# Cross-attention block with MLP: VectorE's transposes in a row, and the plan of the fills dealt anew

## The chip, the cores and the metric

One core of a Trainium2 chip runs the whole kernel in one launch. The metric is the device time of the launch in microseconds. Everything is float32.

## The reference

Four batches of 512 query rows and 512 context rows, width 512, 16 heads of 32, an MLP of 2048:

```python
x = layer_norm(hidden, ln1_w, ln1_b)
q = (x @ q_w + q_b)          # 16 heads of 32
k = (ctx @ k_w + k_b)
v = (ctx @ v_w + v_b)
scores = einsum('bhqd,bhkd->bhqk', q, k) * scale   # masked keys get the lowest float
out = einsum('bhqk,bhkd->bhqd', softmax(scores), v)
hidden = out @ cproj_w + cproj_b + hidden
y = layer_norm(hidden, ln2_w, ln2_b)
y = gelu_tanh(y @ fc_w + fc_b)
return hidden + (y @ proj_w + proj_b)
```

## The kernel before

**Units, halves, blocks.** A unit `w` is one batch and one group of four heads, so there are 16 units, four to a batch. A block `p` is half a unit: 256 of its 512 query rows. The 32 blocks p0 to p31 run one after the other. In a block (`block`, L279) TensorE makes eight score tiles (`scores`, L254; two tiles of 128 query rows by four heads, each 128x512 in a PSUM bank of its own). VectorE adds the mask and takes the row minimum of the negated scores (`soften`, L265), ScalarE takes the exponential with its row sums (L269), and VectorE transposes the result in 32x32 squares, two heads at a time (`turn`, L277: four such instructions of 128x1024 to a block), and last the reciprocals of the sums (L300).

**Exchange.** The squares are then moved between partitions: GpSimd copies the four quarters that stay where they are (L329), and twelve DMAs carry the other twelve (L335). They are all issued on SyncE's queue; only for the last block every second row of them is issued on ScalarE's. `attend` (L338) multiplies the exchanged probabilities by V two or three blocks later, and VectorE scales the result into `oT` (L357).

**Fills.** What else the kernel has to do is dealt out by hand to the blocks: `put(p, ...)` lists the pieces of block p, and `block` calls `fill(0)`, `fill(1)` and `fill(2)` at three places. A piece has a cost: 3.4 (`CHAIN`) for a chain of matmuls (K, Q or V of a unit, one row tile of the output projection `cproj`, or of the MLP's second product `proj`), 5.95 for a pair of columns of the MLP's first product (`fc_by_pair`, seven products in place of eight), 0.5 for a transpose by TensorE and 0 for loads, statistics and normalizations. `fill(0)` and `fill(1)` take pieces up to a budget of 3.4, where a piece still fits when half its cost does; `fill(2)` takes the rest. So each engine has one fixed order of instructions: the order in which the program names them. Every piece of a fill stands in it between the block's own instructions, on VectorE, ScalarE, GpSimd and SyncE too.

**First layer norm.** For the batches 1 to 3 its three parts (`x2`: two of statistics, one of normalization; `ln1`, L178) and its four transposes (`x3`, `ln1_turn`) are pieces as well. For the batches 1 and 2 ScalarE does the normalization (L145) and copies the transposes out of PSUM (L163).

**MLP weights.** Eight slots of 256 KB form a ring. `load_mlp` (L449) loads the next weight on SyncE's queue as soon as the weight that is in its slot has been used for the last time; the list `weights` gives the order and the last use. `fc_sums` (L532) then lets GpSimd add up the blocks of a pair's weights. The gelus of a pair (L525) follow its last sum directly, on ScalarE.

**Beginning and end.** Ahead of p0 the kernel loads, normalizes batch 0 and makes K, V and Q of unit 0 (L876 to L908). Behind p31 come the rest of the MLP pieces, the last two `attend`s, `cproj` of batch 3 and the remaining MLPs (`last_mlps`), which the change leaves as they are.

Of the kernel before, what the change touches and what calls it, by code (L numbers as in the profile page):

```python
# [12 lines left out]
F32 = mybir.dt.float32  # L13
# [7 lines left out]
P = 128  # L21
# [29 lines left out]
def xattn_block(ctx: ExitStack, tc: tile.TileContext, x, encT, mask, q_w, k_w, v_w, c_w, fc_w, p_w, vecs, rows, out):  # L51
# [60 lines left out]

    S = {}
# [108 lines left out]
    def prep_q(w):  # L222
        b, g = divmod(w, NG)
        qT = k_q(w, 1)
        acc = acc_tile(f"accq_{w}")
        for d in range(ND):
            nc.tensor.matmul(acc, S["wq", w][:, d, :], xT[:, d, :], start=(d == 0), stop=(d == ND - 1))  # L227
        load_w(w + 2, names=("wq",))

        nc.scalar.activation(qT, acc, AF.Identity, bias=qb[:, g : g + 1], scale=-scale)  # L230
        S["qT", w] = qT
# [47 lines left out]
    def block(w, half, fill):  # L279

        q0, q1 = 2 * half, 2 * half + 1
        if half == 0:
            S["sums", w] = small.tile([P, NT, HG], F32, tag="sums", name=f"sums_{w}")
        tb = S["tb", w, half] = two.tile([P, NI, PW + 2 * HD], F32, tag="tb", name=f"tb_{w}_{half}")
        scores(w, q0)
        scores(w, q1)
        soften(w, q0, 0, 1, 2, 3)
        soften(w, q1, 0, 1)
        turn(w, q0, 0)
        soften(w, q1, 2, 3)  # L290
# [9 lines left out]
        nc.vector.transpose(  # L300
            tb[:, :, PW:].rearrange("p j (a q) -> p a j q", a=2), rr.rearrange("p a h d -> p (a h d)")
        )
# [18 lines left out]
    def copies(w, half):  # L321
# [8 lines left out]
        for d in range(1, NI):  # L330
            for i in (0, 2, 1, 3):
                j = (i + d) % NI

                q = nc.scalar if w == NW - 1 and half and i % 2 else nc.sync
                q.dma_start(out=pT[ts(j, HD), i], in_=tb[ts(i, HD), j])  # L335
        S["pT", w, half] = pT
# [89 lines left out]
    def ln2_turn(b, d):  # L426
# [4 lines left out]

    weights, products = [], []
    all_k = range(FQ)
    steps = [(n, 0, q, all_k) for n, q in (
        ("fc", 0), ("fc", 1), ("p", 0), ("fc", 2), ("p", 1), ("fc", 3), ("p", 2)
    )]
    steps += [
        ("fc", SPLIT, 0, (0, 1)), ("p", 0, 3, all_k), ("fc", SPLIT, 0, (2, 3)), ("fc", SPLIT, 1, all_k),
        ("p", SPLIT, 0, all_k), ("p", SPLIT, 1, all_k),
    ]  # L440
    for name, b, q, ks in steps:
        for n, k in enumerate(ks):
            last = len(products) + (n if name == "fc" else NT - 1)
            weights.append((name, b, q * FQ + k, last))
        products += [(name, b, q, k) for k in ks]

# [47 lines left out]

    def fc_seven(b, c, g, a, s, half):

# [12 lines left out]
        product(q1[:, 0], a[0][:, 0:2], y11)  # L509
        nc.scalar.copy(p1, q1[:, 0])  # L510
        product(q26[:, 0], a[0][:, 2:4], y21)
        product(q26[:, 1], s2, t2)
# [8 lines left out]
        add(nc.vector, g[:, 1:3], q34, g[:, 1:3])  # L521
        for i in range(2):
            f = 2 * c + i
            h = g[:, 2 * i : 2 * i + 2]
            nc.scalar.activation(h, h, AF.Gelu_apprx_tanh, bias=vec[:, FCB + f : FCB + f + 1], scale=1.0)  # L525

# [17 lines left out]
    def fc_by_pair(b, c):  # L544
        q, k = divmod(2 * c, FQ)
        fc_seven(b, c, gT[q % 2][:, k : k + 2, :], raw_pair(b, c), S["ws", b, c], acc_half)
        count[1] += 2
        count[4] += 1
        load_mlp()
        fc_sums()  # L550

    def proj(b, q, t):
        acc = acc_tile(f"accp_{b}_{q}_{t}")
        for k in range(FQ):
# [300 lines left out]

    def FC(b, q):
        return [(2 * CHAIN * 7 / 8, lambda c=c: fc_by_pair(b, c)) for c in range(q * FQ // 2, (q + 1) * FQ // 2)]

    def PJ(b, q):
        return [(CHAIN, lambda t=t: proj(b, q, t)) for t in range(NT)]  # L860

    def inputs(b):
# [28 lines left out]
    load_w(1, nc.sync, ("wv", "wq"))  # L891

    load_mlp()

# [5 lines left out]
    run(turns1(0))  # L900
    x1, x2, x3, x4 = inputs(1)
    run(x1)
# [8 lines left out]
    mlp = []  # L911
    mlp += FC(0, 0) + FC(0, 1) + PJ(0, 0) + FC(0, 2) + PJ(0, 1) + FC(0, 3) + PJ(0, 2)
    mlp += FC(SPLIT, 0)[:1] + PJ(0, 3) + FC(SPLIT, 0)[1:] + FC(SPLIT, 1) + PJ(SPLIT, 0) + PJ(SPLIT, 1)

# [31 lines left out]
    def put(p, *work, before=()):  # L946
# [33 lines left out]
    put(14, [q], some(2))  # L980
    put(15, some(2), x2[1:2], some(2))

    k, q, v = A(11)
    put(16, h_(1, 0, 1), x2[2:], [k, q], x3[:2], some(2), x3[2:3])
    put(17, [v], x3[3:], h_(1, 2, 3), x4, cb(1), C(1))
# [35 lines left out]
    exchange()  # L1021

# [61 lines left out]
```

## Time and profile before

| what | value |
|---|---|
| time, median of 3 runs | 776.24 us (775.86 to 776.32) |
| the profiled execution | 776.39 us |
| its span from the first to the last instruction | 774.6 us |
| granted TensorE clock, mean | 0.999 |
| VectorE busy | 622.6 us, 80% of the span |
| ScalarE busy | 338.4 us, 44% |
| GpSimd busy | 298.7 us, 39% |

All times below are microseconds from the first instruction of the profiled execution. A row of the chain of waits has start, duration and what ran; a row of the timeline has start, duration, engine, line, instruction, output and inputs, and in brackets the idle time of the engine before it with what ended it. SPq and ACTq are the queues on which SyncE and ScalarE issue DMAs; the duration is then that of issuing. One matmul of float32 counts as two instructions.

### The profile page before, as it was taken

To read this page: it belongs to the slowest core of one execution; us is meant where nothing else is said; L and a number is where in the kernel's file an instruction comes from. 1 tells how busy PE (TensorE), PEld (TensorE's weight loads), DVE (VectorE), ACT (ScalarE), POOL (GpSimd) and SP (SyncE) were. 2 spreads that over 40 slices of the span, in tenths; PEclk is the share of its full clock that TensorE was granted. 3 is DMA by queue.
4 is the path that set the end of the run, shared out by engine and by line. 5 is a ranking of instruction groups with operands and counts; after the bars stand their busy time and mean duration, and the time that the engine had idled before them with its cause. 6 is when DMAs were issued, how large, how long until landed. Compare 5 with 4: busy or idle time off the path is not lost.

```text
span 774.6 us, 12975 instructions
## 1 busy us (share of the span) xinstructions
PE 767.5 (99%) x4442; PEld 519.3 (67%) x4442; DVE 622.6 (80%) x1262; ACT 338.4 (44%) x760; POOL 298.7 (39%) x311
## 2 busy tenths in 40 slices
PE   9999999999999999999999999999999999999998
PEld 6655555467754745565554556446888889988897
DVE  3798999787988857877887889877878999679863
ACT  2577767477774626547663567401201221012200
POOL 1435446377355364224573553350060024300052
PEclk9999999999999999999999999999999999999999
DMA  8978778457766766664656586783523330023001
GB/s 329 309 223 216 183 200 229 125 151 177 224 167 162 183 181 169 156 173 121 162 136 189 144 240 167 207 254 122 199 84 98 90 115 14 28 83 95 1 16 41
DMA packets 54818, 119.37 MB, mean 154 GB/s; under 512 B 10417, under 2 KB 13617, under 8 KB 54625
## 3 DMA queue, kind: packets, MB, share of 16 engines
q1 hardware_dynamic: 53424, 114.88, 53.3%
q0 software_dynamic: 896, 2.82, 1.2%
q10 hardware_dynamic: 432, 0.86, 0.5%
q8 instruction: 35, 0.57, 0.3%
q14 instruction: 31, 0.25, 0.1%
HBM read 58.22 MB, written 6.82 MB: 84 GB/s over the span
## 4 chain that ended last, share of the span: by engine, by line
PE 96%; DVE 2%; DMA 1%; SPq 0%; issue 0%; ACT 0%; ACTq 0%; POOL 0%; DVEq 0%; POOLq 0%
PE q L507 25%; PE accp L555 9%; PE sc L259 8%; PE accv L239 8%; PE acck L217 7%; PE r L645 7%; PE accq L227 7%; PE av L352 7%; PE accc L392 7%; PE q4p L682 2%; PE q1p L700 2%; PE tp L158 2%; PE q2p L682 1%; DMA xe<-tb 1%; DVE tb L277 1%; PE warm L888 1%
## 5 line engine op out<-in xcount | busy, mean ns | idle before, releaser
L269 ACT ACTIVATE ptt<-ptt,mn 128x512 f32<-128x512 f32 x256 | 181.6, 710 | 125.8 <-DVE mn L265 125.8
L265 DVE CUSTOM_DVE_ANT_0 ptt<-sc,mb 128x512 f32<-128x512 f32 x256 | 161.5, 687 | 21.5 <-PE sc L259 16.9
L277 DVE STREAM_TRANSPOSE tb<-ptt 128x1024 f32<-128x1024 f32 x128 | 155.1, 1221 | 0.0
L329 POOL COPY pT<-tb 32x1088 f32<-32x1088 f32 x96 | 104.3, 1087 | 52.8 <-DVE oT L357 32.8
L555 PE MATMUL accp<-pbt,gt 128*128 128x512 f32 x192 | 85.1, 597 | 0.0
L507 PE MATMUL q<-yT,gt 128*128 128x256 f32 x320 | 78.9, 379 | 0.0
L259 PE MATMUL sc<-pbt 32*128 32x512 f32 x512 | 70.7, 616 | 1.5 <-ACT pbt L230 0.8
L555 PEld LDWEIGHTS accp<-pbt,gt 128*128 128x128 f32 x192 | 35.7, 190 | 47.6 <-issue 39.7
L507 PEld LDWEIGHTS q<-yT,gt 128*128 128x128 f32 x320 | 60.8, 190 | 8.7 <-issue 0.5
L525 ACT ACTIVATE ga<-ga,vec 128x512 f32<-128x512 f32 x40 | 26.7, 714 | 87.9 <-DVE ga L467 87.9
L239 PEld LDWEIGHTS accv<-ptt,xe 128*128 128x128 f32 x512 | 59.0, 192 | 8.4 <-DVE mn L265 5.3
L507 PE MATMUL q<-ys,gt 128*128 128x256 f32 x240 | 61.7, 379 | 0.0
L239 PE MATMUL accv<-ptt,xe 128*128 128x128 f32 x512 | 60.2, 276 | 0.0
L217 PE MATMUL acck<-xe,ptt 128*128 128x512 f32 x128 | 58.7, 601 | 0.0
L227 PE MATMUL accq<-xe,ptt 128*128 128x512 f32 x128 | 58.2, 597 | 0.0
L392 PE MATMUL accc<-wc,oT 128*128 128x512 f32 x128 | 56.1, 595 | 0.0
L507 PEld LDWEIGHTS q<-ys,gt 128*128 128x128 f32 x240 | 45.5, 190 | 6.6 <-DVE gt L464 0.4
L259 PEld LDWEIGHTS sc<-pbt 32*128 32x128 f32 x512 | 28.5, 183 | 30.9 <-issue 17.0
L269 ACT ACTIVATION_READ_ACCUMULATOR ptt<-ptt,mn 128x1 f32 x256 | 47.8, 187 | 0.0
L352 PE MATMUL av<-pT,v 128*32 128x256 f32 x768 | 46.4, 382 | 0.0
L217 PEld LDWEIGHTS acck<-xe,ptt 128*128 128x128 f32 x128 | 23.5, 192 | 31.0 <-issue 22.5
L251 POOL TENSOR_TENSOR v<-v,row 128x512 f32<-128x512 f32 x16 | 20.3, 1272 | 61.5 <-ACT v L244 61.5
(179 smaller groups left out, 1187.1 us busy)
## 6 DMA issues: line engine op xcount, KB each, us to landing
pT<-tb SPq DMA_DIRECT2D x288, 136.0 KB, 2.4
pbt<-p_w_dram SPq DMA_DIRECT2D x40, 256.0 KB, 3.1
gt<-fc_w_dram SPq DMA_DIRECT2D x40, 256.0 KB, 2.6
gt<-tb SPq DMA_DIRECT2D x48, 136.0 KB, 2.8
pbt<-fc_w_dram SPq DMA_DIRECT2D x24, 256.0 KB, 3.3
xe<-tb SPq DMA_DIRECT2D x42, 136.0 KB, 2.8
ptt<-k_w_dram SPq DMA_DIRECT2D x16, 256.0 KB, 3.9
xe<-encT_dram SPq DMA_DIRECT2D x16, 256.0 KB, 4.0
```

Source lines behind the costliest of these rows:

```text
L217: nc.tensor.matmul(acc, S["wk", w][:, d, :], eT[:, d, :], start=(d == 0), stop=(d == ND - 1))
L227: nc.tensor.matmul(acc, S["wq", w][:, d, :], xT[:, d, :], start=(d == 0), stop=(d == ND - 1))
L239: nc.tensor.matmul(acc[:, ts(t, P)], eT[:, d, ts(t, P)], S["wv", w][:, d, :], start=(d == 0), stop=(d == ND - 1),)
L259: nc.tensor.matmul(S["sc", w, qt][h], qT[r, ts(qt, P)], kT[r, :], start=True, stop=True)
L265: nc.vector.tensor_tensor_reduce(out=s, in0=S["sc", w, qt][h], in1=S["mb", w // NG], scale=1.0, scalar=FMAX, op0=ALU.add, op1=ALU.min, acc ...
L269: nc.scalar.activation(s, s, AF.Exp, bias=mn, scale=-1.0, accum_out=S["sums", w][:, qt, h : h + 1])
L277: nc.vector.transpose(tv[:, qt % 2, 2 * k : 2 * k + 2], S["ps", w, qt, k])
L329: nc.gpsimd.tensor_copy(pT[ts(i, HD), i], tb[ts(i, HD), i])
L352: nc.tensor.matmul(av[ts(h, HD), : 2 * P].rearrange(shape, **kw), v[:, t, ts(h, HD)], p[t][h], start=(t == 0), stop=(t == NT - 1),)
L392: nc.tensor.matmul(acc, S["oT", b][:, g, ts(t, P)], wc[:, g, :], start=(g == 0), stop=(g == NG - 1))
L507: nc.tensor.matmul(o, x[:, k], y[:, k], start=(k == 0), stop=(k == 1))
L555: nc.tensor.matmul(acc, gT[q % 2][:, k, ts(t, P)], S["pw", b, q * FQ + k], start=(k == 0), stop=(k == FQ - 1))
```

## The change

1. In `block`, the second transpose of the first row tile comes directly behind the first, ahead of the last two `soften`s; `fill(1)` comes behind all transposes, where it stood ahead of the last. `fill(0)` is left out where the block's first piece is a pair of the MLP. In the last block the exchange is issued ahead of `fill(1)`, and wholly on SyncE's queue.
2. The gelus of a pair wait in a list. They are called behind the next pair's first copy, ahead of a `proj` that works on the same buffer, or at the end of the block.
3. Q of unit 0 is made in two halves of 256 columns.
4. x of batch 1 is loaded into `gt` at the start, where the first eight MLP weights were loaded; its statistics come ahead of Q of unit 0, its normalization into p0. The eight weights are loaded behind `wc`.
5. `weights` and the MLP pieces come from one list, `products`, in which single row tiles of `proj` can be placed.
6. The plan (`put`) is dealt anew: Q of unit 4 goes into p4, Q of 5 into p5, Q of 6 into p6, K of 7 into p7, Q and V of 7 into p8, which leaves p9 without V of 7; the statistics of batch 2 go behind `cproj` of row tile 1 in p9; the second layer norm's statistics of batch 1 all go into p20; the MLP pieces of p26 to p31 are 3, 3, 4, 3, 3, 2 chains, where they were 4, 3, 3, 4, 3, 3, and four are left for the end, where two were.

```diff
@@ prep_q
-        acc = acc_tile(f"accq_{w}")
-        for d in range(ND):
-            nc.tensor.matmul(acc, S["wq", w][:, d, :], xT[:, d, :], start=(d == 0), stop=(d == ND - 1))
+        parts = [slice(0, L)] if w else [slice(0, 2 * P), slice(2 * P, L)]
+        for c in parts:
+            acc = acc_tile(f"accq_{w}_{c.start}")[:, c]
+            for d in range(ND):
+                nc.tensor.matmul(acc, S["wq", w][:, d, :], xT[:, d, c], start=(d == 0), stop=(d == ND - 1))
+            nc.scalar.activation(qT[:, c], acc, AF.Identity, bias=qb[:, g : g + 1], scale=-scale)
...
@@ block
         turn(w, q0, 0)
+        turn(w, q0, 1)
         soften(w, q1, 2, 3)
         fill(0)
-        turn(w, q0, 1)
+        turn(w, q1, 0)
...
-        turn(w, q1, 0)
-        fill(1)
         turn(w, q1, 1)
         nc.vector.transpose(
             tb[:, :, PW:].rearrange("p j (a q) -> p a j q", a=2), rr.rearrange("p a h d -> p (a h d)")
         )
         waiting.append((w, half))
-        if w < NW - 1 or half == 0:
+        last = w == NW - 1 and half
+        if last:
+            exchange()
+        fill(1)
+        if not last:
             exchange()
         fill(2)
+        gelus()
@@ copies
-                q = nc.scalar if w == NW - 1 and half and i % 2 else nc.sync
-                q.dma_start(out=pT[ts(j, HD), i], in_=tb[ts(i, HD), j])
+                nc.sync.dma_start(out=pT[ts(j, HD), i], in_=tb[ts(i, HD), j])
@@ the MLP's list
+    products = fcs(0, 0, 1, 2, 3) + pjs(0, 0) + fcs(0, 4, 5) + pjs(0, 1) + fcs(0, 6, 7) + pjs(0, 2)
+    products += pjs(0, 3, 0) + fcs(SPLIT, 0) + pjs(0, 3, 1, 2, 3) + fcs(SPLIT, 1, 2) + pjs(SPLIT, 0, 0)
+    products += fcs(SPLIT, 3) + pjs(SPLIT, 0, 1, 2, 3) + pjs(SPLIT, 1)
+    last_use, done = {}, 0
+    for name, b, i, *_ in products:
+        n = 2 if name == "fc" else FQ
+        done += 2 if name == "fc" else 1
+        last_use |= {(name, b, f): done - 1 for f in range(i * n, (i + 1) * n)}
+    weights = [(*k, n) for k, n in last_use.items()]
@@ gelus
+    def gelus(q=None):
+        while S["gelu"] and q in (None, S["gelu"][0][0]):
+            S["gelu"].pop(0)[1]()
...
         product(q1[:, 0], a[0][:, 0:2], y11)
         nc.scalar.copy(p1, q1[:, 0])
+        gelus()
@@ the start
-    load_mlp()
+    for t in range(NT):
+        nc.sync.dma_start(out=gt[:, ts(t, D)], in_=x[1, ts(t, P), :])
...
     nc.sync.dma_start(out=wc, in_=c_w)
+    load_mlp()
     make_mb(0)
...
+    for t in range(NT):
+        ln_stat((1, 1), t, gt[:, ts(t, D)])
+    ln_rs((1, 1))
     prep_q(0)
@@ the plan
-    put(0, [(CHAIN, lambda: prep_v(1)), v2, k2], x2[:1])
-    put(1, [k3, (0.0, lambda: prep_q(1)), (CHAIN, lambda: (prep_v(3), load_enc(1)))], x2[1:2])
-    put(2, [q2], x2[2:], [k4])
+    put(0, [(CHAIN, lambda: prep_v(1)), v2, k2], do(lambda: norm1(1, *range(NT))))
+    put(1, [k3, (0.0, lambda: prep_q(1)), (CHAIN, lambda: (prep_v(3), load_enc(1)))])
+    put(2, [q2], [k4])
     put(3, [q3, v4])
-    put(4, x3[:2], [k5], x3[2:])
-    put(5, [v5, q4])
-    put(6, [q5, k6])
+    put(4, x3[:2], [k5], x3[2:], [q4])
+    put(5, [v5, q5])
+    put(6, [k6, q6])
...
-    put(7, [v6, q6], cb(0))
-    put(8, x1, [k, q])
-    put(9, [v], x4, x2[:2], do(lambda: attend(3, 1)), c[:1], x2[2:], stat(0, 0), c[1:2], stat(0, 1),
+    put(7, [v6, k], cb(0))
+    put(8, x1, [q, v], x4)
+    put(9, c[:1], do(lambda: attend(3, 1)), c[1:2], stat(0, 0), x2[:2], x2[2:], stat(0, 1),
         c[2:3], stat(0, 2), x3, c[3:], stat(0, 3), rs(0))
...
-    put(15, some(2), x2[1:2], some(2))
+    put(15, some(2), x2[1:2], some(1), x2[2:], some(1))
...
-    put(20, [k, q], some(2), stat(1, 0, 1))
-    put(21, [v], some(2), stat(1, 2, 3), rs(1))
+    put(20, [k, q], stat(1, 0, 1, 2, 3), rs(1), some(2))
+    put(21, [v], some(2))
...
-    put(26, some(4))
+    put(26, some(3))
     put(27, some(3))
-    put(28, some(3))
-    put(29, some(4))
+    put(28, some(4))
+    put(29, some(3))
     put(30, hid_(1, 2, 3), some(3))
-    put(31, some(3))
+    put(31, some(2))
...
         def fill(n, work=fills[p]):
-            run(work, CHAIN if n < 2 else None)
+            if n or not work or work[0][0] <= CHAIN:
+                run(work, CHAIN if n < 2 else None)
...
-    run(some(1) + stat(2, 2, 3) + rs(2) + cb(B - 1) + norm(2, 0, 1) + some(1))
+    run(some(2) + stat(2, 2, 3) + rs(2) + cb(B - 1) + norm(2, 0, 1) + some(2))
```

More of the change, by code (lines that the diff above doesn't have):

```diff
@@ L429, in ln2_turn, with fcs, pjs @@
         ln_turn((2, b), d, S["yn", b], S["yT", b])
[L432 to L445, printed above, removed]
+    def fcs(b, *cs):
+        return [("fc", b, c) for c in cs]
+    def pjs(b, q, *ts_):
+        return [("p", b, q, t) for t in ts_ or range(NT)]
+    products = fcs(0, 0, 1, 2, 3) + pjs(0, 0) + fcs(0, 4, 5) + pjs(0, 1) + fcs(0, 6, 7) + pjs(0, 2)
[7 more added lines that the diff above has]
+    weights = [(*k, n) for k, n in last_use.items()]
     weights += [("p", SPLIT, FIRST * FQ + k, None) for k in range(MW)]
@@ L521, in fc_seven, with gelu @@
         add(nc.vector, g[:, 1:3], q34, g[:, 1:3])
[L522 to L525, printed above, removed]
+        def gelu():
+            for i in range(2):
+                f = 2 * c + i
+                h = g[:, 2 * i : 2 * i + 2]
+                nc.scalar.activation(h, h, AF.Gelu_apprx_tanh, bias=vec[:, FCB + f : FCB + f + 1], scale=1.0)
+        S["gelu"].append((q, gelu))
+        if q is None:
+            gelus()
     fc_pairs = [(0, c) for c in range(NP)] + [(SPLIT, c) for c in range(FIRST * FQ // 2)]
@@ L552, in proj @@
     def proj(b, q, t):
+        gelus(q % 2)
         acc = acc_tile(f"accp_{b}_{q}_{t}")
@@ L854, in turns2 @@
         return [(TURN, lambda d=d: ln2_turn(b, d)) for d in range(ND)]
[L856 to L860, printed above, removed]
     def inputs(b):
@@ L900, in xattn_block, with norm1 @@
     run(turns1(0))
-    x1, x2, x3, x4 = inputs(1)
-    run(x1)
     load_h(0, *range(NT))
     nc.sync.dma_start(out=wc, in_=c_w)
+    load_mlp()
     make_mb(0)
     nc.vector.tensor_scalar(qb, vec[:, QB : QB + NG], 0.0, -scale, ALU.add, ALU.mult)
+    for t in range(NT):
+        ln_stat((1, 1), t, gt[:, ts(t, D)])
+    ln_rs((1, 1))
     prep_q(0)
     v_bias(0)
-    mlp = []
-    mlp += FC(0, 0) + FC(0, 1) + PJ(0, 0) + FC(0, 2) + PJ(0, 1) + FC(0, 3) + PJ(0, 2)
-    mlp += FC(SPLIT, 0)[:1] + PJ(0, 3) + FC(SPLIT, 0)[1:] + FC(SPLIT, 1) + PJ(SPLIT, 0) + PJ(SPLIT, 1)
+    def norm1(b, *ts_):
+        for t in ts_:
+            S["xn", b][t] = tiles.tile([P, D], F32, tag="xn", name=f"xn1_{b}_{t}")
+            ln_norm((1, b), t, S["xn", b][t], gt[:, ts(t, D)])
+    S["xn", 1] = [None] * NT
+    x3 = turns1(1)
+    mlp = [
+        (2 * CHAIN * 7 / 8, lambda i=i: fc_by_pair(*i)) if name == "fc" else (CHAIN, lambda i=i: proj(*i))
+        for name, *i in products
+    ]
     def some(n):
```

10 lines of the change are left out of this document (4 added, 6 removed).

## The prediction

> **What bounds the kernel now.** I read the page's busy times first, then the chain of waits, then the timelines of single engines where pieces move.
>
> ```profile
> PE 767.5 (99%) x4442; PEld 519.3 (67%) x4442; DVE 622.6 (80%) x1262; ACT 338.4 (44%) x760; POOL 298.7 (39%) x311
> ```
> ```profile
> PE sc L259 <- ACT pbt L230: 0.8, 1, 0.8
> ```
>
> TensorE is the bound: 99% busy, and the longest waits that it is charged with are about a microsecond, one of them 0.8 for the first Q. A busy matmul row can hide a wait, though. In the chain of waits (start, duration, what) a block's eight score products take 1.93; where `sc` is longer, TensorE stood waiting for a PSUM bank that VectorE or ScalarE had still to empty:
>
> ```profile
> core 0 of [0], span 774.6 us
> ...
> 58.24 3.19 PE sc L259 x16
> ...
> 77.26 0.87 PE tp L158 x8
> 78.13 1.86 PE av L352 x32
> 80.00 3.62 PE sc L259 x16
> ...
> 125.79 1.93 PE sc L259 x16
> 127.72 3.77 PE accv L239 x32
> ...
> 143.85 1.75 PE tp L158 x16
> ...
> 163.46 1.75 PE tp L158 x16
> ...
> 477.69 2.86 PE sc L259 x16
> ...
> 505.44 0.60 ACTq L335
> ```
>
> All such stretches between the first (58.24, excess 1.26) and the last (477.69, excess 0.93) come to about 7.2: 1.26 in p3, 1.69 in p5 (3.62 less 1.93), 0.4 in p8 and 3.9 in four blocks from p21 to p30. With 0.8 at the first Q and 0.9 at the last exchange that is 8.9 of 774.6: the whole that can be won while TensorE's work stays as it is. The profiled execution took 776.39, 1.8 over its span and 0.15 over the median of the three runs, so sums against it stand for the median too.
>
> **The parts that win.** Q in halves: the copy of the first half (part of the 0.8) runs beside the second half's matmuls, -0.75; if the scores wait for the whole of Q after all, 0. Batch 1's normalization leaves p2, where it delayed the reciprocals' copy and so p3's scores: -1.26. Its new place in p0 and its statistics ahead of p0 lie beside idle ScalarE and VectorE time; without that cover they would cost back at most the 1.26. Q of unit 4 moves into p4, so that TensorE has more work there than VectorE and p5's wait goes: -1.69. In p20 to p22 and p26 to p31 statistics and pairs are dealt more evenly: of the 3.9 I let 0.8 stand, since p27 and p29 now end with VectorE's sums behind its transposes, -3.1. GpSimd's weight sums and the pairs' weights still come ahead of their use there, so I cost those moves at nothing. The first MLP loads and x of batch 1 change places on SyncE's queue with the same bytes ahead of the next weights: nothing. The gelus wait no longer in front of ScalarE's next copy; where they now end a block, VectorE's next softenings cover them: nothing, with the loss among the rivals.
>
> **p4.** One stretch of VectorE, from p9, has the prices of what moves there:
>
> ```profile
> 139.02 0.65 DVE L393 TENSOR_TENSOR h<-accc,h 128x512 f32<-128x512 f32 x1
> 139.71 0.69 DVE L127 BATCH_NORM_STATS2 st<-h 128x6 f32<-128x512 f32 x1
> 140.44 0.18 DVE L128 BATCH_NORM_AGGREGATE mv<-st 128x2 f32<-128x6 f32 x1
> 140.54 1.21 DVE L277 STREAM_TRANSPOSE tb<-ptt 128x1024 f32<-128x1024 f32 x1
> 141.67 0.40 DVE L300 STREAM_TRANSPOSE tb<-rr 128x256 f32<-128x256 f32 x1
> ```
>
> What follows a transpose starts 1.13 behind it (140.54 to 141.67). In p4 the transposes of batch 1 are copied out of PSUM by ScalarE, behind the block's eight exponentials:
>
> ```profile
> 78.80 1.43 ACT L163 ACTIVATE xe<-tp,vec 128x512 f32<-128x512 f32 x2
> ```
>
> Two transposes of VectorE's now stand ahead of the last two softenings, not one, which puts those, the last two exponentials and all that follows them on ScalarE off by 1.1. So the first copy starts at 79.9 and ends at 80.65. The new chain, Q of unit 4, needs that copy, and TensorE is ready for it at 78.13, where the transposes end. It waits 2.5 there and some more for the second pair of copies: +2.6, bounds 1.4 (no shift of ScalarE) and 3.2.
>
> **p9.** Here batch 2's statistics move. In the old order they came in `fill(0)`:
>
> ```profile
> 136.54 0.19 POOL L133 TENSOR_SCALAR ve<-mv 128x4 f32<-128x4 f32 x1 [0.47 <-DVE mv L128]
> ```
> ```profile
> 138.44 2.93 ACT L145 ACTIVATE xn<-xn,nm,rs 128x512 f32<-128x512 f32 x4
> ...
> 160.54 2.93 ACT L145 ACTIVATE xn<-h,nm,rs 128x512 f32<-128x512 f32 x4
> ```
>
> The last statistic was there at 136.5, the normalization ran to 141.4, and the transposes on TensorE began at 143.85: a cover of 2.5. What VectorE now does ahead of the statistics costs, by the rows of VectorE under p4: three transposes 3.4, the reciprocals' 0.4, two sums of `cproj` 1.3, one scaling 0.3 and one statistic with its aggregate 0.8, together 6.2. TensorE in turn comes to the transposes earlier: V of unit 7 (the 3.77 at 127.72) has left p9, while three of `cproj`'s row tiles stand ahead of them as before: 3.8 sooner. So 6.2 + 3.8 - 2.5 = 7.5; the first few of the sixteen transposes get done while it waits, so +7.2. Bounds: 3.7 (V's leaving counted at nothing) and 7.5. Nothing hides it: the next piece in TensorE's order is `cproj` of row tile 3, behind these transposes. In p10 the old normalization of the second layer norm ended at 163.47, just as the transposes began (163.46); it shifts by the 1.1 of p4's reasoning: +1.1, bounds 0 and 1.2.
>
> **The end.** SyncE's queue keeps its order:
>
> ```profile
> 33.39 8.64 SPq L335 DMA_DIRECT2D pT<-tb  x12
> 42.14 1.02 SPq L210 DMA_DIRECT2D ptt<-k_w_dram  x2
> ```
>
> The K weights at 42.14 could have had their slot since K of unit 2, the last piece of p0; they were issued when the twelve DMAs of an exchange were through (33.39 + 8.64). In the new list the weights of `proj(1, 1, ...)` are numbers 44 to 47, and 46 and 47 take the slots of 38 and 39, weights of `proj(1, 0, ...)`, whose last use is its row tile 3 in `fill(1)` of p31. (In the old list their slots came from a pair of p29.) So these two loads are issued behind the whole last exchange, and `proj(1, 1, 0)`, which follows one `av` later, waits for them with everything behind it on TensorE.
>
> ```profile
> 492.85 2.00 PE L259 MATMUL sc<-pbt 32*128 32x512 f32 x16
> ...
> 515.22 1.93 PE L352 MATMUL av<-xe,v 128*32 128x256 f32 x32 [0.94 <-DMA xe<-tb]
> 517.08 1.13 PE L392 MATMUL accc<-wc,oT 128*128 128x512 f32 x2
> ```
> ```profile
> pbt<-p_w_dram SPq DMA_DIRECT2D x40, 256.0 KB, 3.1
> ```
> ```profile
> 469.88 0.69 DVE L467 TENSOR_TENSOR gt<-q,p 128x512 f32<-128x512 f32 x1 [1.23 <-ACT p L510]
> 470.68 1.95 DVE L467 TENSOR_TENSOR gt<-q,gt 128x512 f32<-128x512 f32 x3
> ```
>
> I count from p31's scores (492.85). The old exchange began at 505.44, 12.6 on; one of the two sums of 0.6 in it now comes later: 12.0. But VectorE comes late out of p30, where the pair's sums (the row above is that of the old p29) stand ahead of the third transpose with a wait for ScalarE's copy: the 11.4 of a bare block, 1.2 of wait, 2.7 of sums, 0.6 for the `proj` and 0.4 for `oT` make 16.3, while TensorE (1.9 of scores, seven eighths of two chains, one chain, `av`) wants its last score bank at 14.4. That is 1.9, bounds 0 and 2.2; the exchange starts at 13.9. Twelve issues at 0.63 (the 0.60 at 505.44 with a gap) end at 21.5, the load lands 3.1 later at 24.6; the rest of that row tile (0.9), three chains of 3.43 and the last `av` (1.9) end at 37.6. The old end was 24.2 (517.08), and one chain more now lies here, 3.4, that the earlier blocks no longer have. 37.6 - 24.2 - 3.4 = 10.0, the old wait of 0.9 taken off already. Bounds 8.1 (nothing late in p30) and 11 (issues as slow as those at 33.39).
>
> The rows speak on the single queue too: 7.6 to issue the twelve, 3.1 for one load to land. The Trainium skill, page "DMA: Bandwidth & Descriptors", section "Issuing engines are not separate DMA queues", says that a second issuing engine saves only the time of issuing, usually small beside the transfer. By it the loss of ScalarE's half would be nearly free, and the sum below 3.8 lower. The rows decide: half of 7.6 is 3.8, and with two queues the end's term would be 6.2.
>
> **TensorE's pace after a long wait.**
>
> ```profile
> 1.35 4.21 PE L888 MATMUL warm<-ident 128*128 128x128 f32 x18 [1.35 <-POOL nhalf L879]
> ```
>
> After the launch eighteen instructions of 128 columns took 4.2; at 127.72 thirty-two took 3.77, so eighteen take 2.1. TensorE began at half its pace and lost 2.1. The later waits of TensorE that the waits view lists are under a microsecond, so whether one of 7 or 9 brings the slow start back lies between 0 and 2.1 each. I take the whole, as the one row behind a long idle time shows it: +4.2 for p9 and the end.
>
> The Trainium skill, page "TensorE: Matmul & The Clock Gate", section "Part 1: The HAM clock gate (the "warmup" mystery)", has the clock halved after an idle window of about 3.4 us and whole again after about as much work. By that both waits would be followed by a slow start, and p4's would not.
>
> **The sum.** -0.75 - 1.26 - 1.69 - 3.1 + 2.6 + 7.2 + 1.1 + 10.0 + 4.2 = +18.3. 776.4 + 18.3 = 794.7.
>
> **The rivals.**
>
> *No second slow start* (the waits are as computed, TensorE at full pace behind them): 790.5. For it: nothing after the launch shows one. Against it: the launch does.
>
> *One of the two long waits is covered.* Were batch 2's normalization in time in p9, 785.4 (without 7.2 and 2.1). Were the two weights in time, 781.7 (without 10.0, 2.1 and the 0.9 that stays). For it: other pieces might start sooner than I read the order. Against: each wait follows from the order of one queue.
>
> *Faster: what is ready passes what waits.* Place: SyncE's queue and VectorE's between p9 and p31. If statistics and loads went ahead as soon as their data and slots are there, both long waits would vanish, the small losses of p4 and p10 (3.7) and the end's 0.9 would stay or go as counted, and the wins of 6.8 decide: 776.4 - 6.8 + 3.7 - 0.9 = 772.4. It decides from the point where both waits together are under 3. The row at 42.14 is against it.
>
> *Slower still: the last two softenings, 1.1 later, hold their banks and ScalarE's copies back in every block.* Blocks with two chains give TensorE about 10.9 of work (1.9 + 0.2 + two chains + `av`), where bare VectorE needs some 10.5 to 11; if 0.5 goes lost in ten such blocks, 799.7. For it: the excess at 80.00 is of that kind. Against: in a count of eight banks the next block's scores come to those two last.
>
> **How the numbers follow.** Chances: 0.47 for 794.7, 0.22 without slow starts, 0.15 with one wait covered, 0.05 for faster, 0.11 for slower still. The range of 783 to 800 takes in the first two, the bounds of p4, p9 and the end, most of the slower rival and half of the covered cases. About 0.2% (1.6 us) is what a measurement here can tell from no change. Faster by more than that: 0.05; within it: 0.01; slower: 0.94.
>
> **What would show it.** In the profile after: `tp` in p9 behind a wait of some 7 on ScalarE's normalization, and `accp` in the last rows ahead of `cproj` behind a wait of some 9 on a DMA of `p_w`, issued behind twelve `xe<-tb`; `accq` in p4 waiting for ScalarE's copies; `sc` of p3, p5 and p22 back at 1.93; `sc` directly behind the first `accq`. TensorE's busy share would fall to about 97%. I am wrong if the DMA of those weights is issued ahead of the exchange, or if the statistics in p9 end before TensorE comes to the transposes.

## The result, and the profile after

The changed kernel takes 795.50 us (median of 4 runs, 794.24 to 797.79), the kernel before 776.28 (775.86 to 776.47): ratio 1.0252, 95% interval 1.0228 to 1.0275. The forecast was 794.7 with a range of 783 to 800. The profiled execution took 797.79 us at a span of 794.2, which is 3.6 outside the span where the kernel before had 1.8; so below I compare spans and blocks, 794.2 with 774.6.

The page of the changed kernel, busy times and granted clock by slice:

```profile
PE 771.3 (97%) x4450; PEld 522.0 (66%) x4450; DVE 620.2 (78%) x1262; ACT 340.5 (43%) x763; POOL 299.1 (38%) x311
...
PEclk9999999899999999999999999989999999999999
```

TensorE has 3.8 us more busy time though its matmuls are the same but for Q's halves, and its share falls from 99 to 97%. The clock row has two slices below 9, where it had none. What TensorE waits for (total, times, longest) names the places:

```profile
PE accp L572 <- DMA pbt<-p_w_dram: 7.5, 1, 7.5
PE tp L158 <- ACT xn L145: 6.0, 5, 5.0
PE accq L229 <- ACT xe L163: 2.3, 1, 2.3
PE av L356 <- DMA pT<-tb: 1.7, 1, 1.7
```

The first three are the waits that the prediction named: the end, p9 and p4. The timeline of TensorE shows what came behind them (start, duration, count; in brackets the idle time before):

```profile
79.17 5.40 PE L229 MATMUL accq<-xe,ptt 128*128 128x512 f32 x8 [2.35 <-ACT xe L163]
...
137.67 7.13 PE L396 MATMUL accc<-wc,oT 128*128 128x512 f32 x16
149.76 0.47 PE L158 MATMUL tp<-ident,xn 128*128 128x128 f32 x1 [4.96 <-ACT xn L145]
...
510.52 1.98 PE L572 MATMUL accp<-pbt,gt 128*128 128x512 f32 x4
519.99 14.27 PE L572 MATMUL accp<-pbt,gt 128*128 128x512 f32 x28 [7.49 <-DMA pbt<-p_w_dram]
```

Eight instructions of `accq` take 5.40 behind their wait, where such a chain takes 3.60 at full pace. The same in a table of stretches (from:to, length, then busy time and count of PE, PEld, DVE, ACT and POOL, the granted clock, DMA share and GB/s):

```profile
80.00:85.00 5.00, 5.00 (x19) 1.82 (x22) 0.45 (x1) 2.40 (x5) 0.00 (x0) 0.66 0.02 3
...
150.00:155.00 5.00, 4.31 (x17) 3.49 (x17) 0.00 (x0) 4.21 (x7) 0.00 (x0) 0.50 0.00 0
...
520.00:525.00 5.00, 5.00 (x7) 2.19 (x8) 0.69 (x1) 0.00 (x0) 0.00 (x0) 0.59 0.95 321
```

Each long wait is followed by some microseconds at about half the clock. On SyncE's queue the order at the end is the predicted one, twelve copies of the exchange and then the weights:

```profile
509.52 7.49 SPq L339 DMA_DIRECT2D xe<-tb  x12
517.11 2.91 SPq L461 DMA_DIRECT2D pbt<-p_w_dram  x6
```

And in the chain of waits the score products of p3, p5 and p22 are short again (1.93, where p3 had 3.19 and p5 3.62):

```profile
58.19 1.93 PE sc L260 x16
...
86.44 1.93 PE sc L260 x16
...
359.14 1.93 PE sc L260 x16
```

Block by block, from score product to score product, without the three chains that only changed their block (Q of unit 4 into p4, V of unit 7 out of p9, one chain of `proj` from p26 to p30 into the end):

| place | predicted | measured |
|---|---|---|
| first Q, with p2 | -0.75 | -0.05 |
| p3 | -1.26 | -1.26 |
| p4 | +2.6 | +4.32 |
| p5 | -1.69 | -1.69 |
| p9, with its slow pace | +9.3 | +8.87 |
| p10 | +1.1 | +0.84 |
| p20 to p30 | -3.1 | -3.18 |
| end, with its slow pace | +12.1 | +11.84 |
| the rest | 0 | +0.24 |
| sum | +18.3 | +19.93 |

The moved chains leave -0.34 (V takes 3.77, Q 3.43), so the span grows by 19.6. The lines for p9, p4 and the end hold a stretch at half clock, whose price differs from profile to profile (experiment 8 and the last section).

### The profile page after: what moved, and what is told of

Same layout as the page of the kernel before. It is cut to its first block, busy times and chain, and to the rows that moved or that the text cites. A ratio compares the mean times of both kernels' runs of the same rounds, so it can differ in the third digit from the quotient of the medians.

```text
span 794.2 us, 13002 instructions
## 1 busy us (share of the span) xinstructions
PE 771.3 (97%) x4450; PEld 522.0 (66%) x4450; DVE 620.2 (78%) x1262; ACT 340.5 (43%) x763; POOL 299.1 (38%) x311
## 4 chain that ended last, share of the span: by engine, by line
PE 88%; DVE 5%; ACT 3%; issue 1%; SPq 1%; DMA 1%; POOL 0%; DVEq 0%; ACTq 0%; POOLq 0%
PE q L516 24%; PE accp L572 9%; PE sc L260 7%; PE r L662 7%; PE accv L240 7%; PE accq L229 7%; PE av L356 7%; PE acck L217 6%; PE accc L396 6%; PE q4p L699 2%; PE q1p L717 2%; DVE ptt L266 2%; PE tp L158 2%; PE q2p L699 1%; DVE tb L278 1%; ACT ptt L270 1%
## 5 line engine op out<-in xcount | busy, mean ns | idle before, releaser
L572 PE MATMUL accp<-pbt,gt 128*128 128x512 f32 x192 | 87.3, 608 | 7.5 <-DMA pbt<-p_w_dram 7.5
L260 PE MATMUL sc<-pbt 32*128 32x512 f32 x512 | 66.1, 614 | 0.0
L229 PE MATMUL accq<-xe,ptt 128*128 128x512 f32 (+1 forms) x136 | 60.1, 587 | 2.3 <-ACT xe L163 2.3
L229 PEld LDWEIGHTS accq<-xe,ptt 128*128 128x128 f32 x136 | 25.5, 194 | 33.3 <-issue 22.0
L396 PEld LDWEIGHTS accc<-wc,oT 128*128 128x128 f32 x128 | 24.1, 192 | 30.3 <-issue 27.2
```

Source lines behind the costliest of these rows:

```text
L229: nc.tensor.matmul(acc, S["wq", w][:, d, :], xT[:, d, c], start=(d == 0), stop=(d == ND - 1))
L260: nc.tensor.matmul(S["sc", w, qt][h], qT[r, ts(qt, P)], kT[r, :], start=True, stop=True)
L396: nc.tensor.matmul(acc, S["oT", b][:, g, ts(t, P)], wc[:, g, :], start=(g == 0), stop=(g == NG - 1))
L572: nc.tensor.matmul(acc, gT[q % 2][:, k, ts(t, P)], S["pw", b, q * FQ + k], start=(k == 0), stop=(k == FQ - 1))
```

## The experiments

Every run stands beside the kernel before on the same chip. Ratios, with their intervals, are to that, and where a run is said to take so much less or more than another kernel, that is the difference of their ratios times 776.3 us. The changed kernel's own is 1.0252 [1.0228, 1.0275].

**1. The end: order of the weights.**

```
     weights = [(*k, n) for k, n in last_use.items()]
+    f13 = [w for w in weights if w[:2] == ("fc", SPLIT) and w[2] in (6, 7)]
+    weights = [w for w in weights if w not in f13]
+    at = [w[:3] for w in weights].index(("p", SPLIT, 0))
+    weights[at:at] = f13
```

> The changed kernel with one thing different: in the list of weights the two of the first layer's last pair of the third MLP part (numbers 42 and 43) stand ahead of the four of the second layer's product before (38 to 41), so that the last product's two weights 46 and 47 take the buffers of that pair, which come free a block earlier, and are issued before the last exchange instead of behind its twelve issues on SyncE. Theory (the late loads are what makes the end long, the exchange itself is not): the wait of 7.5 us in the product that reads them and the slow restart behind it go, and the 1.7 us wait of the last two attend products may stay; from 495.6 to the start of the output projection of the last batch about 11 to 12 us less, so 783 to 785 us in all (ratio to the kernel before 1.009 to 1.012). Rival (twelve copies on one queue set the end, whatever stands behind them): the wait moves from the product to the attend product, and the time stays above 792.

Measured: 784.83 us, 1.0106 [1.0092, 1.0120], so 11.3 us less. TensorE's timeline of this run:

```profile
506.92 1.93 PE L356 MATMUL av<-pT,v 128*32 128x256 f32 x32 [0.54 <-DMA pT<-tb]
508.78 14.00 PE L576 MATMUL accp<-pbt,gt 128*128 128x512 f32 x32
```

The 32 instructions run without a gap, in 14.00, and the part behind p31's scores is 10.9 shorter. All but about 1 us of the end's term lies in which buffers two weights take. The last exchange is still issued on one queue, and nothing waits for it.

**2. Block 9: statistics first, TensorE's transposes last.**

```
-    put(9, c[:1], do(lambda: attend(3, 1)), c[1:2], stat(0, 0), x2[:2], x2[2:], stat(0, 1),
-        c[2:3], stat(0, 2), x3, c[3:], stat(0, 3), rs(0))
+    put(9, x2[:2], c[:1], do(lambda: attend(3, 1)), c[1:2], stat(0, 0), x2[2:], stat(0, 1),
+        c[2:3], stat(0, 2), c[3:], stat(0, 3), rs(0), x3)
```

> The changed kernel with one thing different: in block 9 the fill begins with two of the input transposes and takes the four layer-norm statistics one after each output projection, with the last input transposes at its end. Theory (TensorE's 5.1 us wait in block 9 is for ScalarE's normalised inputs, queued behind the block's exponentials and statistics, and the 3 us of half pace behind it are its consequence): the wait and the half pace go, 8 to 9 us less, 786.5 to 787.5 us. Rival (VectorE or ScalarE are simply full there, since V's chain of 3.8 us was moved out of this block): the wait moves to a later instruction of block 9 or 10 and under 3 us are gained, 792.5 or more.

Measured: 787.53 us, 1.0139 [1.0125, 1.0153], 8.8 us less. With batch 2's statistics in the first filling again and one more `cproj` chain ahead of the transposes, these run back to back:

```profile
136.69 10.57 PE L396 MATMUL accc<-wc,oT 128*128 128x512 f32 x24
147.09 1.91 PE L158 MATMUL tp<-ident,xn 128*128 128x128 f32 x16
```

Block 9 takes 21.53 instead of 30.21. With this order V's leaving costs nothing. The edit did two things, the statistics sooner and the transposes one chain later; how much each brings was not tried singly.

**3. Block 4: V of unit 5 instead of Q of unit 4.**

```
-    put(4, x3[:2], [k5], x3[2:], [q4])
-    put(5, [v5, q5])
+    put(4, x3[:2], [k5], x3[2:], [v5])
+    put(5, [q4, q5])
```

> The changed kernel with one thing different: V of unit 5 and Q of unit 4 change places, V in block 4 behind the input transposes and Q with the next Q in block 5. Theory: block 4's wait of 2.6 us for ScalarE's last copy of the transposed inputs goes, since V reads the other input, and so does the slower start of the product behind it (5.40 us instead of 3.43): 4.3 us less, 791 us. Rival (the pace of that product was low for a reason of its own, and the wait comes back in block 5): 0 to 2 us less, 793.5 or more.

Measured: 793.07 us, 1.0214 [1.0199, 1.0230], 2.9 us less. V reads the encoder's rows and not the copies:

```profile
76.92 3.74 PE L240 MATMUL accv<-ptt,xe 128*128 128x128 f32 x32
```

In the profile block 4 is 4.17 shorter, as the theory has it. The time fell by somewhat less, within what the intervals leave open; the block's slow pace, which is part of it, did not show in every profile of the other runs (last section).

**4. The block's order alone, in the kernel before.**

```
         turn(w, q0, 0)
+        turn(w, q0, 1)
         soften(w, q1, 2, 3)
         fill(0)
-        turn(w, q0, 1)
+        turn(w, q1, 0)
...
-        turn(w, q1, 0)
-        fill(1)
         turn(w, q1, 1)
...
         waiting.append((w, half))
+        fill(1)
         if w < NW - 1 or half == 0:
             exchange()
```

> The kernel before with only the order inside a block changed: the transposes of the weights in a row ahead of the second filling, the filling behind them; everything else (places of K, Q and V, loads, gelus, exchange on two queues, order of the weights) as before. Theory (the reorder of VectorE and ScalarE work is hidden behind TensorE in the 32 blocks, its loss lies in the places named): 775 to 779 us, ratio 0.998 to 1.004. Rival (in every block the fillings' additions and the next copies of banks come 1 us later, and TensorE waits for a bank each time): 5 us or more, above 781 us.

Measured: 780.69 us, 1.0055 [1.0042, 1.0068], 4.3 us more: between the two, and my theory's range missed it. The loss is neither hidden everywhere nor paid in every block. It sits in p3, p5, p10 and p16 with 0.83 to 0.88 each, in p30 with 0.62 and at the end with 1.3; p8, p22 and p29 gain 0.26 to 0.72. What p3's late scores wait for, on TensorE and then on ScalarE:

```profile
60.78 1.32 PE L259 MATMUL sc<-pbt 32*128 32x512 f32 x4 [0.82 <-ACT pbt L219]
```
```profile
56.94 2.92 ACT L145 ACTIVATE xn<-xn,nm,rs 128x512 f32<-128x512 f32 x4
59.75 0.39 ACT L297 COPY rr<-rsum 128x256 f32<-128x256 f32 x1
60.05 0.68 ACT L219 ACTIVATE pbt<-acck,vec 128x512 f32<-128x512 f32 x1
```

It is ScalarE's copy of K of unit 4, which stands behind batch 1's normalization. These scores do not read that K, which p8 needs; what they can want of the copy is the PSUM bank that it empties. In the changed kernel K of unit 4 is made in p2 as before, but the normalization has left p2, and p4 has a chain more: there p3 and p5 do not show the wait (1.93 above). So other parts of the change cover this one, by the plan and the rows; it was not tried part by part.

**5. The three edits together**, nothing new in the code.

> The three edits of the experiments on the end, on block 9 and on block 4 together, nothing else different from the changed kernel. Theory (the three places are separate losses, each a wait of TensorE of its own): the gains add, 11.3 + 8.8 + 2.9 = 23 us off 795.5 (each by its ratio to the kernel before), 772.5 us, ratio 0.994 to 0.997, faster than the kernel before. Rival (one loss hides behind another, as a wait that a late stage would have absorbed anyway): 777 us or more, ratio above 1.000.

Measured: 772.35 us, 0.9943 [0.9929, 0.9956]. From 1.0252 that is 24.0 us, against 23.0 for the sum of the three: the losses were separate, and without them the change is faster than the kernel before by 4.4 us. The wait that is left (waits view):

```profile
PE av L356 <- DMA pT<-tb: 2.1, 1, 2.1
```

**6. The last exchange on two queues again, in the changed kernel.**

```
-                nc.sync.dma_start(out=pT[ts(j, HD), i], in_=tb[ts(i, HD), j])
+                q = nc.scalar if w == NW - 1 and half and i % 2 else nc.sync
+                q.dma_start(out=pT[ts(j, HD), i], in_=tb[ts(i, HD), j])
```

> The changed kernel with one thing different: every second copy of the last exchange is issued by ScalarE again, as in the kernel before. By the rows (twelve issues of 0.63 us on SyncE, then the late weights' loads at 517.11): six fewer issues ahead of the loads, which start 3.8 us sooner, so 3.8 us less, 791.5 to 792 us. Rival (what the Trainium skill, DMA: Bandwidth & Descriptors, Issuing engines are not separate DMA queues, says: a second queue only saves issue time, usually small): under 1 us, 794.5 or more.

Measured: 795.70 us, 1.0245 [1.0231, 1.0259]: no gain. The queues of SyncE and ScalarE in this run:

```profile
509.19 6.49 SPq L340 DMA_DIRECT2D xe<-tb  x6
515.78 3.20 SPq L462 DMA_DIRECT2D pbt<-p_w_dram  x6
```
```profile
509.21 5.08 ACTq L340 DMA_DIRECT2D xe<-tb  x6
```

SyncE has half the copies to issue and takes 6.49 for them, not 3.8; ScalarE takes 5.08. The waits of SyncE's queue between 508 and 516 say where 1.8 of the 6.49 went:

```profile
SPq L340 <- DMA xe<-tb: 1.8, 1, 1.8
```

Ahead of its last copy SyncE waited until another copy had landed, by the chain of waits one of ScalarE's (issued at 510.75, landed at 515.16). Without that wait a copy took 0.78 on SyncE and 0.85 on ScalarE, where one queue alone took 0.62. Counted from the first copy, the weights' loads start 1.0 sooner and the product behind them 0.7. That product then takes 15.03 for its 28 instructions instead of 14.27, so in these two profiles its slow start takes back what the loads had gained. The median time from issue to landing (last column) grew as well, first the changed kernel, then this run:

```profile
xe<-tb SPq DMA_DIRECT2D x12, 136.0 KB, 2.4
```
```profile
xe<-tb SPq DMA_DIRECT2D x6, 136.0 KB, 3.8
xe<-tb ACTq DMA_DIRECT2D x6, 136.0 KB, 4.2
```

The Trainium skill, page "DMA: Bandwidth & Descriptors", section "Issuing engines are not separate DMA queues", has the DMAs of all issuing engines run on the same DMA engines, so that a second issuing engine saves only time of issuing, usually little. The trace agrees that it is little: of the 7.5 us of issuing the second queue saved about one. That copies of one queue wait for those of the other, and that each takes longer to issue, is what the trace adds; why was not tried.

**7. and 8. TensorE kept busy through its waits.** The loops stand ahead of block 9's transposes, of Q of unit 4 and of `proj(1, 1, 0)`; what they write is overwritten by the products behind them.

```
+        if key == (1, 2) and d == 0:
+            for _ in range(12):
+                nc.tensor.matmul(tp, ident, row[:, 0, :], start=True, stop=True)
...
+            for _ in range(6 if w == 4 else 0):
+                nc.tensor.matmul(acc, ident, row[:, 0, :], start=True, stop=True)
...
+        if (b, q, t) == (SPLIT, 1, 0):
+            for _ in range(18):
+                nc.tensor.matmul(acc, ident, row[:, 0, :], start=True, stop=True)
```

> The changed kernel with TensorE kept busy during its three waits: products of the identity with a constant row, whose results are overwritten, are put ahead of the waiting instruction, 6 in block 4 (2.6 us), 12 in block 9 (5.1 us) and 18 before the last product's first tile (7.7 us); the waits themselves stay as long. It prices the half pace behind a wait by itself. Theory (the clock falls because TensorE had stood still): the half pace goes at all three places, 0.5 to 1.8 us in block 4, 2 to 3 us in block 9, 2.2 us at the end, 5 to 7 us in all, 788.5 to 790.5 us. Rival (the pace behind the waits is low because operands come late, or because of the load's rise itself): no gain or a loss, 795 us or more.

Measured: 802.92 us, 1.0332 [1.0318, 1.0347], 6.2 us more. I had mis-sized the fillers: such a product is two instructions of 0.43.

```profile
81.10 3.60 PE L234 MATMUL accq<-xe,ptt 128*128 128x512 f32 x8
...
144.76 10.46 PE L159 MATMUL tp<-row,ident 128*128 128x512 f32 x24
```

Twelve of them took 10.46 in a wait of 5. The pace behind them was full, though (3.60 for the chain of `accq`, not 5.40). So with half as many, 6, 3 and 9:

> The kernel of the experiment with fillers in TensorE's waits, with half as many of them. There one product of 128 by 512 turned out to take 0.86 us (two instructions of 0.43), not the 0.43 that their number was reckoned by, so that 12 of them took 10.3 us where the wait was 5.1: the half pace behind the waits was gone, and the fillers' own excess cost more. Now 3 in block 4 (2.6 us), 6 in block 9 (5.1) and 9 at the end (7.7). Theory (standing still is what lowers the pace behind a wait): the same full pace behind them as there, but no excess, so 0.5 to 1.8 us less in block 4, 2 to 3 in block 9 and 2.2 at the end, 789 to 791 us. Rival (the full pace came only since the fillers outlasted the waits by far): 794 us or more.

Measured: 790.95 us, 1.0182 [1.0168, 1.0195], 5.4 us less than the changed kernel, though the loads and copies come as late as there. The stretches that had 0.66, 0.50 and 0.59, and the product at the end:

```profile
80.00:85.00 5.00, 4.77 (x25) 1.83 (x28) 1.27 (x2) 3.59 (x7) 0.00 (x0) 1.00 0.09 31
...
150.00:155.00 5.00, 4.03 (x20) 2.69 (x21) 0.00 (x0) 4.36 (x7) 0.00 (x0) 1.00 0.00 0
...
520.00:525.00 5.00, 5.00 (x13) 2.13 (x12) 2.22 (x5) 0.00 (x0) 0.00 (x0) 1.00 0.89 323
```
```profile
518.01 12.26 PE L580 MATMUL accp<-pbt,gt 128*128 128x512 f32 x28 [0.72 <-DMA pbt<-p_w_dram]
```

The 28 instructions take 12.26 instead of 14.27, block 9 is 1.7 shorter and block 4 1.2. Standing still lowered the pace: that is shown, since with the fillers the clock stays at 1.00. Against the changed kernel's profile its price was 1.2 in block 4, 1.7 in block 9 and 2.0 at the end. These prices vary without any filler: block 9 took 29.70 to 30.95 in the profiles of experiments 1, 3, 6 and 9, and the 28 instructions at the end took 14.91 and 15.03 in those of experiments 2 and 6.

**9. Gelus at once, in the changed kernel.**

```
-        fc_seven(b, c, gT[q % 2][:, k : k + 2, :], raw_pair(b, c), S["ws", b, c], acc_half, q % 2)
+        fc_seven(b, c, gT[q % 2][:, k : k + 2, :], raw_pair(b, c), S["ws", b, c], acc_half)
```

> The changed kernel with one thing different: the gelus of a pair of the first layer stand at once behind its sums, as in the kernel before, not behind the next pair's first copy. Theory (blocks 21 to 30 became 3.2 us shorter, moved products aside, because ScalarE's copy of the next pair is no longer queued behind two gelus): 2 to 3 us more, 797.5 to 799 us, all in blocks with first-layer pairs. Rival (the new order of products, or the transposes in a row, shortened those blocks): no change, 795 to 796 us.

Measured: 796.67 us, 1.0252 [1.0238, 1.0266]: nothing, and blocks 21 to 30 are as long as in the changed kernel, each within 0.02. My theory here fell; putting the gelus off neither costs nor brings anything measurable.

**10. The old order of transposes, with the three edits.** The edit is that of experiment 4 backwards, on the kernel of experiment 5.

> The kernel with the three edits, but inside a block the old order again: the fillings between VectorE's transposes, as in the kernel before. Theory (the transposes in a row cost where a copy of K is due a block later, and K a block sooner has covered that here, but for block 10's 0.84): 1 us less to 0.5 us more, 771.3 to 773. Rival (the transposes in a row, and not the new order of products, are what made blocks 21 to 30 3.2 us shorter): 2 to 3 us more, 774.5 to 775.5.

Measured: 773.44 us, 0.9956 [0.9944, 0.9969], which overlaps with 0.9943: the transposes in a row decide nothing in sum here. In place they do. Block 10's transposes run through with the old order and wait with the new (this run, then experiment 5):

```profile
159.57 1.91 PE L158 MATMUL tp<-ident,xn 128*128 128x128 f32 x16
```
```profile
161.29 1.64 PE L158 MATMUL tp<-ident,xn 128*128 128x128 f32 x13 [0.38 <-ACT xn L145]
```

That block is 0.83 shorter with the old order; p8, p28 and p30 are 0.26 to 0.36 longer. With the old order p20 to p30 are still 2.7 shorter than in the kernel before, so at most 0.5 of the 3.2 is from the new one. With experiment 9 that leaves the new dealing of statistics, pairs and row tiles, by exclusion; it was not tried by itself.

**11. Block 30's pair behind the transposes, with the three edits.**

```
-    put(30, hid_(1, 2, 3), some(3))
+    put(30, some(2), hid_(1, 2, 3), some(1))
```

> The kernel with the three edits and one more: in block 30 the loads of the residual rows stand behind the first layer's pair instead of ahead of it, so that the pair falls into the second filling, and VectorE's sums of the pair (2.7 us and 1.2 of waiting for their copy) come behind the transposes. Theory (block 30's exchange starts 3.9 us late for these sums, and TensorE's 2.2 us wait for it in the attend product of that pair, and the late score banks of block 31, 1.2 us, are its price): the exchange starts at about 481 instead of 484.99, both waits go, 2.5 to 3.5 us less, 769 to 770 us. Rival (twelve copies on the queue end as late as before, or block 31 is bound by VectorE in any case): under 0.5 us, 772 us or more.

Measured: 770.33 us, 0.9919 [0.9905, 0.9932], 1.9 us less than experiment 5 and the fastest of all, though the two intervals just overlap (0.9929 to 0.9932). The exchange of block 30 and what waited for it, in experiment 5 and then here:

```profile
484.99 9.03 SPq L339 DMA_DIRECT2D pT<-tb  x12
```
```profile
483.72 3.32 PE L260 MATMUL sc<-pbt 32*128 32x512 f32 x16
...
496.16 1.94 PE L356 MATMUL av<-pT,v 128*32 128x256 f32 x32 [2.05 <-DMA pT<-tb]
```
```profile
480.57 7.50 SPq L339 DMA_DIRECT2D pT<-tb  x12
```
```profile
483.28 2.00 PE L260 MATMUL sc<-pbt 32*128 32x512 f32 x16
...
492.27 1.93 PE L356 MATMUL av<-pT,v 128*32 128x256 f32 x32
```

It starts 4.4 sooner, the scores of p31 are whole again and `av` does not wait. In the profile both waits are gone and the part behind p31's scores is 3.4 shorter. The time gained less than the 2.5 to 3.5 expected. A likely reason is that the wait of `av` varies from run to run: the profiled execution of experiment 5 was the slowest of its five by 1.0 to 2.2.

**12. The first Q whole, with the three edits.**

```
-        parts = [slice(0, L)] if w else [slice(0, 2 * P), slice(2 * P, L)]
+        parts = [slice(0, L)]
```

> The kernel with the three edits, but with the first Q whole again, one product and one copy, as in the kernel before. Theory (the half microsecond won at the first scores is given back in block 2, whose K chain waits for the second batch's encoder rows to land): the first scores 0.5 to 0.8 us later, block 2 shorter by about as much where its chain had waited, the start of block 3 and the whole within 0.4 us, 772 to 773 us. Rival (as the prediction had it): 0.75 us more, all of it kept to the end, 773.1 us.

Measured: 771.41 us, 0.9935 [0.9921, 0.9948], which overlaps with 0.9943: no loss. From the first matmul of Q to the first scores the halves take 3.70 and the whole 4.38, experiment 5 first:

```profile
18.54 3.77 PE L229 MATMUL accq<-xe,ptt 128*128 128x256 f32 x16
22.24 2.00 PE L260 MATMUL sc<-pbt 32*128 32x512 f32 x16
```
```profile
17.15 3.60 PE L229 MATMUL accq<-xe,ptt 128*128 128x512 f32 x8
21.53 2.00 PE L260 MATMUL sc<-pbt 32*128 32x512 f32 x16 [0.78 <-ACT pbt L230]
```

So 0.68 is won in place, but Q itself started between 17.15 and 18.54 from profile to profile, and that swamps it. Block 2 took 10.86 in both, so my theory that it gives the gain back is not borne out here. It stays open, though: block 2 took 11.29 in the changed kernel and up to 12.41 in other profiles with the halves (experiment 9).

## Why the prediction was right

**p9, the end and the sum.** All three long waits of TensorE came where each was put, and for its reason: normalizations behind statistics that VectorE reaches late, two weights behind twelve copies on one queue, a Q chain that needs ScalarE's copies. Experiments 1, 2 and 3 took them away one by one, and experiment 5 shows that they add up. By the prediction's own count from p31's scores, at 496.56 here, the exchange began at 13.0 (13.9 was forecast) and the weights' product went on at 23.4 (24.6).

**The slow restart.** 2.1 was taken for each long wait from the one row after the launch; experiment 8 measured 1.7 and 2.0. The rival without it (790.5) is nearly what experiment 8 ran as a kernel, at 790.95. The whole 2.1 for each was about right, but the price is not fixed: the profiles without fillers put it between 1.2 and 2.5 in block 9 and between 2.0 and 2.8 at the end behind a wait of 6.5 to 7.5. With 1.7 taken off, p9's own wait comes to 7.2, as forecast: 5.0 of it ahead of the first transpose, the rest while the transposes come one by one behind their normalizations. The end's comes to 9.8, forecast 10.0. There some luck helped: the product went on 1.2 sooner than forecast, and the work behind it took 1.1 more at full pace (12.26 in experiment 8) than the 0.9 and three chains of 3.43 that were counted.

**p4 was under-sized**, 4.3 instead of 2.6. The wait itself is right: 2.35 by the profile, and in experiments 2 and 6, where the pace behind it stayed full, 0.23 more for the second pair of copies. The step that failed is that its pace was left at full: the chain behind it took 5.40 for 3.60. At full pace the block takes 1.2 less (16.05); where the other 0.5 lies was not followed. Here the profile and the Trainium skill differ: page "TensorE: Matmul & The Clock Gate", section "Part 1: The HAM clock gate (the "warmup" mystery)", has the clock halved after an idle window of about 3.4 us, and by that a wait of 2.35 would cost no pace. The granted clock of 0.66 behind it says that less idle time than that can be enough.

**Two queues: wrong.** "With two queues the end's term would be 6.2" was a step that the sum did not need, and it failed. Twelve issues on one queue do take 7.5, as reckoned; the mistake was to give six on each of two queues half of that. The trace of before had the rows, and I did not read them:

```profile
507.90 4.18 SPq L335 DMA_DIRECT2D xe<-tb  x6
```
```profile
505.44 4.17 ACTq L335 DMA_DIRECT2D xe<-tb  x6
```

Six took 4.2 there, and from the first issue (505.44) to the end of the last (512.08) passed 6.6, since SyncE's first copy had to wait as well. The waits of SyncE's queue between 504 and 513 in the kernel before say for what:

```profile
SPq L335 <- DMA xe<-tb: 7.1, 1, 7.1
```

It had been idle for 7.1, and its first copy began when ScalarE's first had landed, 2.5 behind that one's issue. So the single queue stands rightly in the forecast, and only the price put on giving up the second one was wrong: about 1 us, not 3.8. Nor would the sum have come out 3.8 lower with that loss nearly free, since the twelve issues on one queue take their 7.5 in any case.

**The first Q** was sized right in place (0.68 for 0.75) and gave nothing that the whole time shows.

**p20 to p30** came out right in size (3.2 for 3.1). That the gelus' new place costs nothing is shown; which of the new dealings shortened these blocks was only narrowed down.

**The slower rival**, late softenings in every block, did not come: experiment 4 shows the later order costing 0.83 to 0.88 in four blocks, and of these four only p10 still shows it in the changed kernel (0.84). By the plan, batch 1's normalization has left p2 ahead of p3, batch 3's has left p16, and p4 has a chain more ahead of p5.

## What to carry to other kernels

When an order is rearranged, follow each moved load to the buffer it takes: two weights that fell behind one exchange cost 11 us, and a swap of list entries gave it back. Reckon a wait of TensorE with what follows it at half pace, 1 to 3 us each here, and judge an edit part by part before it is thrown away: this one loses 2.5% as a whole and wins 0.8% (770.33 us) once four things change places. A second issuing queue is worth what the trace shows with both at work, not half of one queue's time.

## What the runs showed of the hardware that was not expected

A TensorE wait of only 2.35 us could be followed by a chain at reduced pace (granted clock 0.66 over the next 5 us), and the cost varied: block 4 took 17.25 us in the changed kernel and in experiments 1 and 9, 16.05 in experiments 2 and 6, with the same wait. The traces' records of the clock hint at why. Apart from one at each kernel's end, the stretches at half clock last 3.41, 6.83 or 10.24 us, once, twice or three times the same length, and those of the changed kernel begin at 80.33, 148.59 and 517.23, 20 and then 108 such lengths apart. So the clock seems to go by a fixed grid of 3.41 us. Laid on that grid, block 4's wait lies with at least 2.25 us in one step of it in the three profiles with the slow pace, and with at most 1.95 in the two without. That is an inference from five profiles; no run moved the wait on purpose.

Filler matmuls in the waits are worth their place: the kernel with them is 5.4 us faster though it does more work and its data come no sooner.

With two queues issuing the same exchange, one issue took 0.70 us (the kernel before) or 0.78 to 0.85 (experiment 6, without SyncE's wait of 1.8) instead of 0.62, and in experiment 6 landing took 3.8 to 4.2 us instead of 2.4. In both kernels SyncE also stood until a copy had landed before it issued its next.
